# Seventy-three stores of a fused attention and feed-forward kernel, issued by GpSimd instead of SyncE

## The chip, the core and the metric

The kernel runs on one core of one Trainium2 chip. Time is device time in microseconds (us) of one execution; lower is better. Three runs before the change gave 1566.15, 1566.42 and 1566.45 us. All tensors are f32.

A core has five engines that the text calls by short names: PE (TensorE, matrix products), DVE (VectorE), ACT (ScalarE), POOL (GpSimd) and SP (SyncE, which here only starts transfers). Each engine takes its own instructions strictly in order, and waits on semaphores where it needs another engine's work. Transfers between SBUF and DRAM are run by 16 DMA engines; an engine's queue only starts them.

## The reference, cut to what matters

For x of shape (8, 512, 512), eight batches of 512 tokens by 512 features:

```python
xn = layernorm(x)
# attention: q, k, v = xn @ W.T + b; phi = elu + 1 on q and k
kv = cumsum(phi_k * v, axis=tokens)
s  = (phi_q * kv) * 32**-0.5 @ Wo.T + bo
# feed-forward: 512 -> 2048 -> 512 with Walsh-Hadamard transforms
h  = fwht(xn * SU_ug) / 64
h  = silu(h @ Wgate.T * scale_gate) * (h @ Wup.T * scale_up)
f  = fwht(h * SU_dp) / 64 @ Wdown.T * scale
out = x + s * silu(f)
```

The transforms are folded into the weights once, on the chip: a Hadamard transform of the input is the same as one of the weight matrix.

## The kernel before

The eight batches are worked on in four **pairs**. Every matrix product is done by a Strassen-Winograd scheme: seven products of half-size blocks in place of eight, at the price of additions on the blocks. Weights, activations and results therefore exist in seven **factors**, called P1 to P7; P1, P2, P7 and P4 come from the four quarters themselves and P5, P6, P3 and P7 are made by four additions or subtractions ("encoding").

**The first pair** is special: it uses the raw weights, folds and encodes them as it goes, and stores the made factors into DRAM. The other three pairs only load those factors. So nearly all the stores of weights happen in the first quarter of the run. In it:

- `first_w` (q, k, v and o weights): raw blocks are loaded by SP (`raw_w` L350, `rows_w` L367), encoded on POOL (L305 to L308), and `keep_w` (L317 to L321) stores them: 8 stores of 896 KB, 128 pieces of 7168 bytes each.
- `folded_w` (gate and up weights, each in 8 blocks `f`): raw load (L350), butterflies on DVE (L930 to L933), the Hadamard product on PE (L939), scaling on ACT (L945), encoding on DVE (L305 to L308).
- `inner_w` (L394 to L416) encodes a pair of folded blocks a second time. It stores three given factors at once (P1, P2, P4) and then makes P5, P6, P3 and P7 on DVE (L408), each stored when made. Each of these stores is 448 KB in 896 pieces of 512 bytes. P7 is written into the same third of the tile as P5 (`t[:, 0]`), so DVE's P7 has to wait until P5's store has landed. There are seven stores for each of gate and up in each of the four units `u`: 56 in all.
- `down`'s weights: `load_down` (L961), butterflies on DVE (L969, L974), Hadamard products on PE (L988), scaling on ACT (L994), and a store of the folded block into `wd_f` (L997): 4 stores of 1 MB in 512-byte pieces. `first_half_down` loads half of it back (L1008), makes the factors on DVE (L93) and stores them (L1018): 1 store of 3.5 MB. `down_w` does the other half block by block: loads (L367), factors on DVE (L93, L333), store (L388): 4 stores of 896 KB.

These 73 stores are the ones the change touches.

**Order.** A framework gives each engine its list of instructions, in the order of an estimated schedule with priorities, and inserts the semaphores. The kernel steers it: `at(place, fn)` sets a step that many PE groups ahead, `later` and `pace` hang small DVE steps behind given DVE instructions, and `background` lowers the priority of what can wait. All transfers but one are started by SP (the exception loads `cols` from ACT's queue). SP takes them in order, so a store that waits for its data holds all loads behind it. POOL starts no transfer: it does elementwise work, in the first pair the encoding of q, k, v and o weights, `v*k` (L716), the encoding of the attention result `co` and of the hidden units `ho` (L297 to L300, L793, L795).

Of the kernel before, what the change touches and what calls it, by code (L numbers as in the profile page):

```python
# [21 lines left out]
def kernel(  # L22
# [27 lines left out]
    nc = tc.nc  # L50
    P = 128
# [34 lines left out]
    def later(us, fn, *args, soon=False):  # L86
        (urgent if soon else idle).append((us, fn, args))
# [228 lines left out]

    def keep_w(name, w):  # L317
        d = dram.tile([P, 2 * 7 * P], F32, tag=f"d_{name}", name=f"d_{name}")
        nc.sync.dma_start(d, w.rearrange("p j s e -> p (j s e)"))
        kept[name] = d  # L320
        return w  # L321

# [33 lines left out]
    def by_factor(w, n=1):  # L356

        w = flat(w) if len(w.shape) == 4 else w
        w = w[:, : 7 * n * 2 * P] if n == 1 else w[:, : n * 2 * P]
        return w.rearrange("p (s e) -> p s e", e=2 * P)  # L360

    def rows_w(w, src, n0, dn):

        for a in range(2):
            for b in range(2):
                n = n0 + b * dn
                nc.sync.dma_start(  # L367
                    w[:, (P1, P2, P7, P4)[2 * a + b]], src[n * P : (n + 1) * P, a * 2 * P : (a + 1) * 2 * P]
                )

    wd_made = [0, 0]
    wd = [dram.tile([P, 7, 4, 2 * P], F32, tag=f"d_down_{h}", name=f"d_down_{h}") for h in range(2)]

    def down_w(u, j):

        t = t8.tile([P, 2, 7, P], F32, tag="t", name=f"wd_{u}_{j}")
        w = by_factor(t)
        rows_w(w, wd_f, u + NU * j, NG)

        def encode():  # L380
            for o, a, b, op in (
                (P5, P7, P4, ALU.add), (P6, P5, P1, ALU.subtract), (P3, P2, P6, ALU.subtract), (P7, P1, P7, ALU.subtract)
            ):
                later(0.5, nc.vector.tensor_tensor, w[:, o], w[:, a], w[:, b], op)
            later(0.0, store)

        def store():
            nc.sync.dma_start(wd[u // 2][:, :, 2 * (u % 2) + j], w)  # L388
            wd_made[u // 2] += 1

        at(8, encode)

    def inner_w(m, u, w0, w1):

        if u not in inner:
            inner[u] = dram.tile([P, 7, 2, 7, P], F32, tag=f"d_gu_{u}", name=f"d_gu_{u}")
        d = inner[u][:, :, ("gate", "up").index(m)]

        def store(c, t):
            nc.sync.dma_start(d[:, :, c, :], t)  # L400

        store(P1, w0[:, 0])
        store(P2, w0[:, 1])
        store(P4, w1[:, 1])
        t = xin.tile([P, 3, 7, P], F32, tag="x", name=f"s_{m}_{u}")

        def made(c, i, a, b, op):
            nc.vector.tensor_tensor(t[:, i], a, b, op)  # L408
            store(c, t[:, i])

        later(1.0, made, P5, 0, w1[:, 0], w1[:, 1], ALU.add, soon=True)
        later(1.0, made, P6, 1, t[:, 0], w0[:, 0], ALU.subtract, soon=True)
        later(1.0, made, P3, 2, w0[:, 1], t[:, 1], ALU.subtract, soon=True)
        later(1.0, made, P7, 0, w0[:, 0], w1[:, 0], ALU.subtract, soon=True)
# [7 lines left out]
    def at(place, fn):  # L422
        agenda.append((now[0] + place, now[1], fn))
        now[1] += 1
# [533 lines left out]
    wd_f = dram.tile([FF, D], F32, tag="wd_f", name="wd_f")  # L958
# [24 lines left out]
    def fold_down(o):  # L983
        r = rs[:, o % 2]
        for a in range(NF // 4):
            p = ps.tile([P, 4, P], F32, tag="t", name=f"pwd_{o}_{a}")
            tc.keep_in_program_order(
                nc.tensor.matmul(  # L988
                    p.rearrange("p c e -> p (c e)"), had,
                    r[:, 4 * a : 4 * a + 4].rearrange("p c e -> p (c e)"), start=True, stop=True,  # L990
                )
            )
            for c in range(4):
                nc.scalar.activation(  # L994
                    r[:, 4 * a + c], p[:, c], AF.Copy, scale=su_dp[:, 4 * a + c : 4 * a + c + 1]
                )
        nc.sync.dma_start(wd_f[:, o * P : (o + 1) * P].rearrange("(c p) e -> p c e", p=P), r)  # L997

    def first_half_down():

        n = 4 * 2 * P
        w = [rd[:, i * n : (i + 1) * n] for i in range(7)]
        for a in range(2):
            for b in range(2):
                t = w[(P1, P2, P7, P4)[2 * a + b]].rearrange("p (u j e) -> u p j e", u=2, j=2)
                d = wd_f[:, a * 2 * P : (a + 1) * 2 * P].rearrange("(b j u p) e -> b u p j e", b=2, j=2, p=P)
                for u in range(2):
                    nc.sync.dma_start(t[u], d[b, u])  # L1008

        def factors():  # L1010
            for i, x, y, op in (
                (P5, P7, P4, ALU.add), (P6, P5, P1, ALU.subtract), (P3, P2, P6, ALU.subtract), (P7, P1, P7, ALU.subtract)
            ):
                later(1.2, nc.vector.tensor_tensor, w[i], w[x], w[y], op, soon=True)
            later(0.0, at, 4, store, soon=True)

        def store():
            nc.sync.dma_start(wd[0].rearrange("p i k e -> p (i k e)"), rd)  # L1018
            wd_made[0] = 4

        at(8, factors)
# [4 lines left out]
    def first_w(m, g):  # L1026


        if m == "gate":
            return folded_w(m, wgate_t, g)  # L1030
        if m == "up":
            return folded_w(m, wup_t, g)
        name, eng = f"{m}_{g}", nc.gpsimd
        if m == "o":
            t = new_w(name)
            w = by_factor(t)
            rows_w(w, wo_t, g, 2)
        else:
            t = w = raw_w(name, sources[m], 0, 2, 1, g * P, 2 * P)

        def encode():
            encode_weights(eng, w)
            keep_w(name, t)

        return w, [(5, encode)]
# [73 lines left out]
    for i in range(7):  # L1119
        dst = had if i % 2 == 0 else had2  # L1120
        s = src.rearrange("p (a t h) -> p a t h", t=2, h=1 << i)
        d = dst.rearrange("p (a t h) -> p a t h", t=2, h=1 << i)
# [16 lines left out]
    rd = hop.tile([P, 2, 7, L], F32, tag="h", name="rd").rearrange("p m s t -> p (m s t)")  # L1139
# [9 lines left out]
    def chain_down(o):  # L1149
        def folded_block():  # L1150
            fold_down(o)
            if o + 2 < KD:
                at(8, lambda: load_down(o + 2))
            if o + 1 == KD:
                at(8, first_half_down)

        def then():
            at(10, folded_block)
            if o + 1 < KD:
                at(4, lambda: chain_down(o + 1))  # L1160

        butterflies_down(o, then)
# [116 lines left out]
```

## Time and profile before

| what | value |
|---|---|
| median of the three runs | 1566.42 us |
| the profiled execution's own time | 1564.62 us |
| span of its instructions | 1562.8 us |
| PE busy | 1529.4 us (98%) |
| DVE busy | 985.1 us (63%) |
| POOL busy | 497.5 us (32%) |
| ACT busy | 418.8 us (27%) |
| PE idle in 0 to 400 us / from 400 us on | 27.7 us / 5.9 us |
| POOL busy in 0 to 400 us | 130.2 us |
| bytes moved | 273.31 MB, mean 175 GB/s |

The page gives each engine's busy time and its share of the span, then 40 equal slices of the span with a digit for the busy tenths. "Waits" list who waited for whom: total us, number of times, longest. A window row gives the busy time of each engine in a stretch, the clock that the throttle granted to TensorE, the share in which the DMA engines were busy, and the GB/s. "To landing" is from a transfer's issue to its last byte's signal. SP's instructions are queue entries and not counted as busy.

### The profile page before, as it was taken

To read this page: it belongs to the slowest core of one execution; us is meant where nothing else is said; L and a number is where in the kernel's file an instruction comes from. 1 tells how busy PE (TensorE), PEld (TensorE's weight loads), DVE (VectorE), ACT (ScalarE), POOL (GpSimd) and SP (SyncE) were. 2 spreads that over 40 slices of the span, in tenths; PEclk is the share of its full clock that TensorE was granted. 3 is DMA by queue.
4 is the path that set the end of the run, shared out by engine and by line. 5 is a ranking of instruction groups with operands and counts; after the bars stand their busy time and mean duration, and the time that the engine had idled before them with its cause. 6 is when DMAs were issued, how large, how long until landed. Compare 5 with 4: busy or idle time off the path is not lost.

```text
span 1562.8 us, 15732 instructions
## 1 busy us (share of the span) xinstructions
PE 1529.4 (98%) x5924; PEld 1127.0 (72%) x5924; DVE 985.1 (63%) x1379; ACT 418.8 (27%) x664; POOL 497.5 (32%) x280
## 2 busy tenths in 40 slices
PE   7999999998999999999999999999999999999998
PEld 3335545845884588888885488888886468888887
DVE  5897785677866674716676574725675476543673
ACT  4443341142114521112215431111212431111211
POOL 4633144004321262304612235301622236110731
PEclk9999999999999999999999999999999999999999
DMA  8244867797785344344575434336474233535462
GB/s 280 78 153 152 268 218 225 232 275 270 200 304 196 91 158 155 108 152 165 157 286 213 102 137 148 135 102 195 153 249 171 85 106 117 185 99 177 155 260 85
DMA packets 197693, 273.31 MB, mean 175 GB/s; under 512 B 56817, under 2 KB 155121, under 8 KB 193393
## 3 DMA queue, kind: packets, MB, share of 16 engines
q1 hardware_dynamic: 197472, 272.27, 53.3%
q8 instruction: 47, 0.77, 0.2%
q14 instruction: 30, 0.24, 0.0%
q10 hardware_dynamic: 144, 0.03, 0.0%
HBM read 196.25 MB, written 76.02 MB: 174 GB/s over the span
## 4 chain that ended last, share of the span: by engine, by line
PE 88%; DVE 4%; DMA 3%; issue 2%; POOL 1%; ACT 1%; SPq 1%; POOLq 0%; DVEq 0%; ACTq 0%
PE px_gu L630 20%; PE px_dn L528 13%; PE pz_gu L630 10%; PE pz_dn L528 6%; PE py_gu L630 5%; PE py_dn L528 4%; PE px_k L452 3%; PE px_v L452 3%; PE px_o L528 3%; PE px_q L452 3%; PE pz_o L528 2%; PE pz_k L452 2%; PE px_gate L452 2%; PE pz_q L452 2%; PE pz_v L452 1%
## 5 line engine op out<-in xcount | busy, mean ns | idle before, releaser
L630 PE MATMUL px_gu<-xo,w_gu 128*128 128x256 f32 x1456 | 348.9, 381 | 0.0
L630 PEld LDWEIGHTS px_gu<-xo,w_gu 128*128 128x128 f32 x1456 | 277.5, 191 | 44.2 <-issue 5.0
L528 PE MATMUL px_dn<-w_down,ho 128*128 128x256 f32 x1024 | 228.9, 379 | 0.0
L528 PEld LDWEIGHTS px_dn<-w_down,ho 128*128 128x128 f32 x1024 | 194.9, 190 | 28.7 <-issue 2.9
L630 PE MATMUL pz_gu<-xo,w_gu 128*128 128x256 f32 x728 | 188.6, 382 | 5.4 <-DVE a L661 5.2
L831 POOL TENSOR_TENSOR u<-u,v 128x1024 f32<-128x1024 f32 x26 | 60.8, 2363 | 371.2 <-DVE u L668 347.5
L630 PEld LDWEIGHTS pz_gu<-xo,w_gu 128*128 128x128 f32 x728 | 138.3, 191 | 26.2 <-DVE a L661 6.1
L528 PE MATMUL pz_dn<-w_down,ho 128*128 128x256 f32 x496 | 112.4, 380 | 3.2 <-DVE u L468 3.2
L528 PEld LDWEIGHTS pz_dn<-w_down,ho 128*128 128x128 f32 x496 | 93.9, 190 | 17.0 <-DVE u L468 3.6
L630 PE MATMUL py_gu<-xo,w_gu 128*128 128x256 f32 x364 | 93.5, 379 | 0.0
L876 POOL TENSOR_TENSOR s<-s,d 128x512 f32<-128x512 f32 x30 | 40.0, 1333 | 165.5 <-ACT d L875 126.4
L716 POOL TENSOR_TENSOR v<-v,k 128x1024 f32<-128x1024 f32 x16 | 43.0, 2685 | 138.9 <-ACT v L691 111.2
L630 PEld LDWEIGHTS py_gu<-xo,w_gu 128*128 128x128 f32 x364 | 69.3, 190 | 9.3
L835 POOL TENSOR_TENSOR v<-v,r 128x1024 f32<-128x1024 f32 x26 | 60.9, 2362 | 27.7 <-DVE r L668 27.7
L793 POOL TENSOR_TENSOR ho<-g,u 128x512 f32<-128x512 f32 x6 | 10.9, 1812 | 161.0 <-DVE u L468 151.1
L452 PE MATMUL px_k<-xo,w_k 128*128 128x512 f32 x128 | 61.6, 603 | 0.0
L452 PE MATMUL px_v<-xo,w_v 128*128 128x512 f32 x128 | 60.8, 595 | 0.0
L821 ACT ACTIVATE a<-a,cols_sb 128x512 f32<-128x512 f32 x26 | 18.8, 722 | 155.2 <-DVE a L668 153.4
L452 PE MATMUL px_q<-xo,w_q 128*128 128x512 f32 x128 | 60.2, 593 | 0.0
L722 DVE TENSOR_TENSOR_SCAN k<-ones,v 128x512 f32<-128x512 f32 x32 | 40.9, 1317 | 28.6 <-POOL v L716 28.6
L528 PE MATMUL px_o<-w_o,co 128*128 128x256 f32 x256 | 58.4, 380 | 0.0
L875 ACT ACTIVATE d<-d 128x512 f32<-128x512 f32 x31 | 19.5, 630 | 144.5 <-DVE d L543 102.4
(264 smaller groups left out, 2476.5 us busy)
## 6 DMA issues: line engine op xcount, KB each, us to landing
w_gu<-d_gu SPq DMA_DIRECT2D x91, 896.0 KB, 4.4
w_down<-d_down SPq DMA_DIRECT2D x56, 512.0 KB, 3.6
d_s<-o SPq DMA_DIRECT2D x8, 1024.0 KB, 4.3
d_d<-dn SPq DMA_DIRECT2D x8, 1024.0 KB, 7.7
d<-d_d SPq DMA_DIRECT2D x8, 1024.0 KB, 6.2
s<-d_s SPq DMA_DIRECT2D x8, 1024.0 KB, 8.1
y<-in_x_dram SPq DMA_DIRECT2D x8, 1024.0 KB, 7.3
out_dram<-y SPq DMA_DIRECT2D x15, 512.0 KB, 3.3
```

What stands on the lines that cost most here:

```text
L452: nc.tensor.matmul(p.rearrange("p a t -> p (a t)") if len(r.shape) == 2 else p, ws[k][:, i, :], r, start=(first and k == 0), stop=(k == n ...
L528: nc.tensor.matmul(p[:, c], t[:, (2 * g + c) * P : (2 * g + c + 1) * P], ws[i](k), start=(first and k == 0 and c == cs[0]), stop=(k == n - ...
L630: nc.tensor.matmul(p[:, lane], w[:, lane, i, :], x[:, i, :], start=(first and lane == 0), stop=True, skip_group_check=True,)
L716: nc.gpsimd.tensor_tensor(v[:, h], v[:, h], k[:, h], ALU.mult)
L722: nc.vector.tensor_tensor_scan(k[:, h, s], ones.to_broadcast([P, L]), v[:, h, s], 0.0, ALU.mult, ALU.add)
L793: nc.gpsimd.tensor_tensor(ho[:, P1], g[:, 0, 0], r[:, 0, 0], ALU.mult)
L821: nc.scalar.activation(g[:, m], g[:, m], AF.Silu, scale=col("w_gate", u + m * NU + a * NG))
L831: nc.gpsimd.tensor_tensor(r[:, m], ru1[:, m], rv[:, m], ALU.add)
L835: nc.gpsimd.tensor_tensor(rv[:, m], rv[:, m], rr[:, m], ALU.add)
L875: nc.scalar.activation(d, d, AF.Silu)
L876: (nc.vector if final and (a, s) == (1, 0) else nc.gpsimd).tensor_tensor(r, r, d, ALU.mult)
```

## The change

Five `dma_start` calls are moved from SyncE's queue to GpSimd's. Nothing else is edited; the data, the sizes and the waits that each store needs are the same. The loads, the stores of normalized `x`, the parked results and the output stay on SyncE.

```diff
     def keep_w(name, w):
         d = dram.tile([P, 2 * 7 * P], F32, tag=f"d_{name}", name=f"d_{name}")
-        nc.sync.dma_start(d, w.rearrange("p j s e -> p (j s e)"))
+        nc.gpsimd.dma_start(d, w.rearrange("p j s e -> p (j s e)"))
...
         def store():                                   # down_w
-            nc.sync.dma_start(wd[u // 2][:, :, 2 * (u % 2) + j], w)
+            nc.gpsimd.dma_start(wd[u // 2][:, :, 2 * (u % 2) + j], w)
...
         def store(c, t):                               # inner_w
-            nc.sync.dma_start(d[:, :, c, :], t)
+            nc.gpsimd.dma_start(d[:, :, c, :], t)
...
-        nc.sync.dma_start(wd_f[:, o * P : (o + 1) * P].rearrange("(c p) e -> p c e", p=P), r)
+        nc.gpsimd.dma_start(wd_f[:, o * P : (o + 1) * P].rearrange("(c p) e -> p c e", p=P), r)
...
         def store():                                   # first_half_down
-            nc.sync.dma_start(wd[0].rearrange("p i k e -> p (i k e)"), rd)
+            nc.gpsimd.dma_start(wd[0].rearrange("p i k e -> p (i k e)"), rd)
```

## The prediction

> **What bounds the kernel now.** I read the page's busy line and slices first, then PE's waits, then the windows around each of them.
>
> ```profile
> PE 1529.4 (98%) x5924; PEld 1127.0 (72%) x5924; DVE 985.1 (63%) x1379; ACT 418.8 (27%) x664; POOL 497.5 (32%) x280
> ...
> PE   7999999998999999999999999999999999999998
> ```
>
> PE is busy for 98% of the span; all that an edit of queues can win is PE's idle time and what the throttle takes after it. The change acts on the first pair only, so the next view is the windows before and after 400 us:
>
> ```profile
> 0.00:400.00 400.00, 372.32 (x1076) 207.01 (x1077) 303.25 (x431) 139.82 (x269) 130.24 (x101) 0.97 0.68 213
> 400.00:1563.00 1163.00, 1157.07 (x4850) 920.01 (x4848) 681.87 (x949) 278.93 (x395) 367.29 (x180) 1.00 0.49 162
> 195.00:275.00 80.00, 76.79 (x211) 39.74 (x210) 57.67 (x81) 24.47 (x44) 36.11 (x21) 1.00 0.71 222
> 380.00:386.80 6.80, 3.72 (x9) 3.00 (x10) 6.52 (x12) 0.00 (x0) 1.82 (x2) 0.58 0.75 294
> ```
>
> The columns are the stretch, its length, busy us of PE, PEld, DVE, ACT and POOL, the granted clock, DMA share and GB/s. PE is idle for 27.7 us of the first 400 (8.3 of them before 40 us, while the first data arrive), and 5.9 us later. The last row shows a second price: after a stall of PE the clock was granted at 0.58 for some microseconds. Who ended PE's waits between 20 and 400 us:
>
> ```profile
> PE pz_gu L630 <- DVE a L661: 5.2, 1, 5.2
> PE pz_q L452 <- DVE q L468: 3.4, 1, 3.4
> PE pz_dn L528 <- DVE u L468: 3.2, 1, 3.2
> PE pwd L988 <- ACT w_gate L945: 3.2, 1, 3.2
> PE pz_o L528 <- DVE g L468: 2.9, 1, 2.9
> ```
>
> Five stalls carry 17.9 us: S1 at 55.9 us (pz_q), S2 at 105.9 (pwd), S3 at 142.9 (pz_o), S4 at 263.2 (pz_dn), S5 at 377.9 (pz_gu). Each time a PSUM bank is not yet read, because DVE or ACT is late. No stall names a transfer, so I ask next what made DVE late (DVE's waits, 0 to 400 us):
>
> ```profile
> DVE s_gate L408 <- DMA d_gu<-s_gate: 7.3, 2, 7.2
> DVE r_gate L930 <- DMA w_gate<-in_wgate_t_dram: 6.5, 2, 5.3
> ...
> DVE r_up L930 <- POOL ho L299: 6.1, 1, 6.1
> ...
> DVE wd L333 <- DMA wd<-wd_f: 4.6, 1, 4.6
> ```
>
> The first is 10 us ahead of S3, the second right ahead of S4, the fourth inside S5. In S5 SP's timeline shows the cause: a store (L388) held the queue until its data were made at 370.1 us, and the loads that DVE needs stood behind it and a second store.
>
> ```profile
> 361.73 0.61 SPq L327 DMA_DIRECT2D w_gu<-d_gu  x1
> 370.18 0.51 SPq L388 DMA_DIRECT2D d_down<-wd  x1
> 370.81 1.72 SPq L367 DMA_DIRECT2D wd<-wd_f  x2
> 372.63 0.52 SPq L388 DMA_DIRECT2D d_down<-wd  x1
> 373.50 1.77 SPq L367 DMA_DIRECT2D wd<-wd_f  x2
> ```
>
> S4 is alike: a store of s_up at 253.7 us waited for DVE, and seven raw loads of w_gate came after it at 255.0.
>
> **What is removed from SP.** 73 issues: 56 of L400 at a median of 0.52 us, 4 of L388 at 0.52, 4 of L997 at 0.37, 9 of L319 and L1018 at 0.34, together 36 us. SP is on no path by these; what counts is the waiting ahead of them.
> - S5: with the two L388 stores gone from the queue the four loads can start after 361.7 us, 9 us sooner, and DVE's wait of 4.6 goes. PE's 5.2 us of idle go, and the clock: PE ran from 383.1 to 386.8 at half speed, 3.7 us for 1.85 us of work. **-7.1.** Late next is DVE itself, which works through the xo and wd subtractions at 362 to 374 us without a wait.
> - S4: the load comes 4.7 us sooner, but P7 of s_up comes later (below). **-2.5.**
> - S3: DVE made P5 of s_gate at 122.1 us and stood at P7 until 132.3, because its store was issued at 125.1, behind two that waited (d_o for POOL, wd_f for ACT), and took 7.2 to land. On POOL it stands behind the last encoding of w_o (ends at 124.2): 124.2 + 2.4 + 3.0 = 129.6, 2.7 us sooner. **-2.7** of S3's 2.9.
> - S1 and S2 hang on v L716, the scans and DVE's order, and on no store.
>
> **What is added to POOL.** The trace of before has no transfer issued by POOL, so its time for one store is the unknown that decides. Below: SP's 0.52 for the same store. Above: 4.4, the median from issue to landing of the d_gu stores, if POOL were held as long as the whole transfer. Between them lies what POOL takes to pass over a tile of about this size, 2.36 (L835, 128x1024; the stored tile is 128x896). I take 2.4 for stores in 512- or 1024-byte pieces, the row nearest in size, and 1.3 (the usual row of 128x512) for the nine in whole rows: 64 x 2.36 + 9 x 1.27 = 162 us on top of the 130 that POOL works in 400 us. Laid out in the order in which data were ready in this trace, with POOL's own instructions at their times:
> - S1: d_v is ready at 45.7, as v L716 wants to start: +1.3 us on the chain v, scan, q to PE. **+1.3** (0.3 to 2.4).
> - Unit 1 (195 to 275 us) issues 14 stores of d_gu and the store of rd: 36.1 + 14 x 2.36 + 1.3 = 70 of 80 us. It fits; the limit is (80 - 36.1 - 1.3) / 14 = 3.0 us a store. From 237 us to L795 at 266.5, eight stores and 11 us of POOL's own work share 29.5 us: no delay up to 2.3 us a store. L795 and its followers L298 to L299 feed down's P2 and later products; PE takes P2 at 275.2 against 269.1 ready, which covers 6 us more.
> - P7 waits for P5's store: 3.0 us from issue to landing at best, plus POOL's time and queue. For s_up of unit 1: ready 247.4, POOL free at 249.9, landed at 255.3, against P7's start at 250.5 before. That is in S4's sum. In the other units DVE waits 0 to 2.5 us more, and waits of that size (3.3 at 219, 3.6 in the scans) preceded no idle of PE.
> - co (L298 to L300) is pushed back by up to 11 us at 126 to 130; PE takes its P6 some 20 us later. ho of unit 2 by 5 us at 362 to 382; POOL then idles for 17 us. Loads of made factors come 30 us or more after their stores (w_gu of unit 3 at 335.6 for use at 364), or in the second pair.
> - Waiting stores now hold POOL's work behind them, as they held SP's. That work (ho, co, v) mostly waits for the same late DVE, so I put it at nothing; where it does not, the price is a late ho, the first rival.
>
> Against the change speaks the Trainium skill, "DMA: Bandwidth & Descriptors", section "Issuing engines are not separate DMA queues": starting transfers from several engines saves only the sequencer's issue time, usually small. By that the gain would be nothing, since SP's 36 us are on no path; S5's row shows a queue that was held by a wait, which the sentence does not count. The same page, section "Latency and other measured facts", gives about 1 us to the first byte for a transfer from GpSimd and 0.6 from SyncE: 0.4 us more on each P7 wait if it holds, and no run here shows it yet.
>
> **The sum.** -7.1 - 2.5 - 2.7 + 1.3 = -11.0 us at 2.36 us a store. The framework will write another order for all engines, since its estimate of two queues changes; the first pair now has five stalls of 3.6 us on average plus some 1.4 of slow clock, and I allow one new one: +5. That gives -6 on the profiled execution's 1564.6, so 1558.6; the median of the three runs lies 1.8 above that execution: **1560.4**, about 1560.
>
> **Rivals.**
> 1. *POOL becomes the late engine* (slower). From 3.0 us a store on, unit 1 does not fit. At 2.8 my layout has L795 6 us late and P7 of s_up 9 us late; S4 stays and grows by 2, w_up's load (held until L795, which ended SP's longest load wait there) and so DVE at r_up by 6 to 10, of which the trace's pattern (6.1 us of such a wait cost nothing) leaves about 8 to PE, plus 3 of clock: with S5 gone about +6, and 1574. At 4.4 the first pair asks 304 + 130 = 434 us of POOL in 385: at least 50 longer, less S5, +40 or more, 1606. For it: 896 pieces a store, and POOL in program order. Against: POOL is idle from 273 to 343 us. Chance 0.32.
> 2. *The landing, not the issue*: stores and loads on two queues share the 16 DMA engines, 0.91 to 0.94 busy at 160 to 200 and 320 to 360 us; P5's stores take 7 us where they took 3 to 4, and DVE stands at P7 in all eight places. At 4 us each, with half of them reaching PE, +16, less 10: +6, 1572. Chance 0.12.
> 3. *Nothing to win*: most of the relief falls into 275 to 335 us, where PE is busy 60 of 60 us, and S4 and S5 come back in a new order. Within 3.1 us of 1566.4. Chance 0.12.
> 4. The forecast: faster, 1550 to 1563. Chance 0.44.
>
> **Range and chances.** A difference under 0.2% (3.1 us) can't be told from none. Faster 0.44; same 0.12; slower 0.32 + 0.12 = 0.44. The low end takes the lower bound of POOL's time (0.52 a store: -15 before the new stall): 1550. The high end takes in rival 1 up to about 4.4 us a store: 1605. The likeliest case alone spans 1550 to 1563.
>
> **What would show it.** In the new trace: POOL's mean for a d_gu store (below 2.5 right, above 3 wrong); the loads of wd at about 362 us and no wait of DVE at L333; no PE idle near 378; DVE's wait at P7 per unit (below 4 right); POOL's ho and co later by less than 10 us. A POOL that never idles in 195 to 275 us would be rival 1; short POOL times with landings of 7 us, rival 2. My sum is wrong at its root if POOL is held by each store's landing, or if the new order moves DVE's steps so that five other stalls appear.

## The result and the profile after

The changed kernel took 1573.57 us (median of 4 runs, 1572.81 to 1576.65) against 1566.43 for the kernel before in the same comparison: the ratio is 1.0044, with an interval of 1.0031 to 1.0057. It is 7.1 us slower where I had forecast 6 us faster. Its profiled execution took 1573.88 us, with a span of 1572.1; that of before took 1564.62.

The busy line of the page, and the stretch of unit 1 with the same columns as before:

```profile
PE 1533.1 (98%) x5924; PEld 1126.3 (72%) x5924; DVE 994.8 (63%) x1379; ACT 418.5 (27%) x664; POOL 562.0 (36%) x353
```

```profile
195.00:275.00 80.00, 72.91 (x180) 34.62 (x179) 62.77 (x79) 20.81 (x35) 41.63 (x33) 0.95 0.59 212
```

GpSimd worked 64.5 us more in all (562.0 against 497.5), and in the stretch from 195 to 275 us it is busy for 41.6 of 80 us: it is not the engine that became the bound. TensorE lost its time there: it was idle for 7.1 us in place of 3.2, and the granted clock fell from 1.00 to 0.95. Who ended PE's waits (20 to 400 us):

```profile
PE pz_o L528 <- DVE g L468: 5.8, 1, 5.8
PE px_gate L452 <- ACT sb_gate L462: 3.4, 1, 3.4
PE pwd L988 <- ACT w_gate L945: 3.2, 1, 3.2
PE pz_gu L630 <- DVE u L468: 3.0, 1, 3.0
PE pz_up L452 <- DVE u L468: 2.8, 2, 1.6
PE pz_q L452 <- DVE q L468: 2.6, 1, 2.6
PE pz_dn L528 <- POOL ho L300: 2.5, 1, 2.5
PE pz_gate L452 <- DVE g L468: 1.6, 1, 1.6
```

Eight groups with 24.9 us stand where five with 17.9 stood. S3 (pz_o) doubled, a stall at 216 us (px_gate) is new, S4 (pz_dn) now names GpSimd, and S5 came back as two smaller ones (pz_up, pz_gu).

TensorE's instructions come in the same order in both kernels, so the two traces can be laid side by side, matmul by matmul. How far the changed kernel lies behind, in us, and what each place added (half clock included):

| place | predicted | in the trace | behind by then |
|---|---|---|---|
| S1 and up to 135 us | +1.3 | -2.3 | -2.3 |
| S3, 135 to 148 us | -2.7 | +4.6 | +2.3 |
| new stall at 216 us | +5 (allowance) | +5.4 | +7.7 |
| S4, 260 to 278 us | -2.5 | +3.5 | +11.2 |
| S5, 375 to 395 us | -7.1 | -2.1 | +9.1 |

After 400 us nothing more is added. The 9.1 is that of the two profiled executions, which lie 9.3 apart; the medians lie 7.1 apart.

VectorE's waits (0 to 400 us) say where it was held:

```profile
DVE s_gate L408 <- DMA d_gu<-s_gate: 8.2, 3, 7.2
DVE r_up L930 <- DMA w_up<-in_wup_t_dram: 7.2, 2, 6.7
...
DVE s_up L408 <- DMA d_gu<-s_gate: 5.1, 1, 5.1
...
DVE s_up L408 <- DMA d_gu<-s_up: 3.7, 2, 3.5
```

The 6.7 us at r_up (until 283.5 us) cost nothing: PE has no stall after it. L408 writes P7 over P5 in the tile of made factors, and the next tile takes the same slot, so VectorE stands until a store has landed. With a group of 1.8 us further down, it did so for 18.8 us; before, the three such groups had 10.4. S3 shows why. GpSimd's timeline first:

```profile
125.37 2.12 POOL L299 TENSOR_TENSOR co<-co 128x512 f32<-128x512 f32 x1
127.43 1.21 POOL L997 DMA_DIRECT2D wd_f<-rd  x1
128.64 2.90 POOL L400 DMA_DIRECT2D d_gu<-s_gate  x3
```

ScalarE had made the data of L997 by 119.5 us and VectorE had made P5 by 122.2, but both stores stand behind the encoding of co (119.1 to 127.4) in GpSimd's order. P5 went out at 128.6 (before: 125.1) and landed at 134.6, and VectorE went on there:

```profile
134.62 1.09 DVE L408 TENSOR_TENSOR s_gate<-w_gate,w_gate 128x896 f32<-128x896 f32 x1 [7.17 <-DMA d_gu<-s_gate]
```

SyncE's timeline shows a second wait beside it:

```profile
104.64 1.78 SPq L367 DMA_DIRECT2D w_o<-in_wo_t_dram  x4
133.24 0.38 SPq L961 DMA_DIRECT2D rd<-in_wdown_t_dram  x1
135.78 7.06 SPq L350 DMA_DIRECT2D w_up<-in_wup_t_dram  x8
```

The queue that was to be freed stands still for 26.7 us: the load of rd (L961) overwrites what L997 stores and waits until it has landed, and the eight loads of w_up stand behind it. They go out at 135.8 us; before it was 135.5.

The wait ahead of the new stall at 216 us is of the first kind. VectorE's timeline:

```profile
196.86 1.09 DVE L408 TENSOR_TENSOR s_up<-w_up,w_up 128x896 f32<-128x896 f32 x1 [3.54 <-DMA d_gu<-s_up]
```

The place S4 needs its clock read beside its stalls. The rows of 260 to 278 us, with the columns of before: the kernel before, the changed kernel, and e5 of the experiments below, in which only L388 was moved:

```profile
260.00:278.00 18.00, 14.79 (x57) 10.47 (x56) 11.80 (x22) 4.39 (x10) 8.04 (x5) 1.00 0.47 139
260.00:278.00 18.00, 14.31 (x45) 9.41 (x44) 15.89 (x15) 0.16 (x1) 10.92 (x10) 0.81 0.52 169
260.00:278.00 18.00, 13.87 (x42) 9.22 (x41) 10.72 (x18) 4.27 (x10) 8.01 (x5) 0.81 0.39 112
```

TensorE's idle time there hardly grew (3.2 us before, 3.7 after). What was added is clock: 0.81 in place of 1.00. The kernel before was spared the half clock at S4, and e5, with every d_gu store still on SyncE, was not.

### The profile page after: what moved, and what is told of

It is laid out like the page before. It is cut to its first block, busy times and chain, and to the rows that moved or that the text cites. A ratio compares the mean times of both kernels' runs of the same rounds, so it can differ in the third digit from the quotient of the medians.

```text
span 1572.1 us, 15823 instructions
## 1 busy us (share of the span) xinstructions
PE 1533.1 (98%) x5924; PEld 1126.3 (72%) x5924; DVE 994.8 (63%) x1379; ACT 418.5 (27%) x664; POOL 562.0 (36%) x353
## 3 DMA queue, kind: packets, MB, share of 16 engines
q1 hardware_dynamic: 133200, 227.70, 44.2%
q0 software_dynamic: 10512, 44.57, 7.4%
## 4 chain that ended last, share of the span: by engine, by line
PE 84%; DVE 7%; DMA 3%; issue 2%; POOL 2%; ACT 1%; SPq 0%; POOLq 0%; DVEq 0%; ACTq 0%
PE px_gu L630 20%; PE px_dn L528 13%; PE pz_gu L630 10%; PE pz_dn L528 6%; PE py_gu L630 5%; PE py_dn L528 4%; PE px_o L528 3%; PE px_k L452 3%; PE px_v L452 3%; PE px_q L452 3%; PE pz_o L528 2%; PE px_gate L452 2%; PE pz_k L452 2%; DVE rd L969 1%; PE pz_q L452 1%
## 5 line engine op out<-in xcount | busy, mean ns | idle before, releaser
L821 ACT ACTIVATE a<-a,cols_sb 128x512 f32<-128x512 f32 x26 | 18.8, 722 | 155.2 <-DVE a L668 153.4
L528 PE MATMUL py_dn<-w_down,ho 128*128 128x256 f32 x256 | 57.9, 379 | 0.0
```

The costliest lines, as they stand in the source:

```text
L528: nc.tensor.matmul(p[:, c], t[:, (2 * g + c) * P : (2 * g + c + 1) * P], ws[i](k), start=(first and k == 0 and c == cs[0]), stop=(k == n - ...
L821: nc.scalar.activation(g[:, m], g[:, m], AF.Silu, scale=col("w_gate", u + m * NU + a * NG))
```

## The experiments

Five theories, by the letters used in the expectations. **A**: VectorE is held by landings of stores of made factors, which GpSimd issues late or which land late. **B**: GpSimd's own encodings stand behind its stores. **C**: only the new written order costs time, whatever the queue. **D**: SyncE stands at a load that waits for a moved store (L961 for L997). **E**, for S5: VectorE has no room at 362 to 385 us, so the stall comes back in another place. In the diffs `sync` and `gpsimd` are the queues. Each kernel was timed beside the kernel before on the same chip, whose median lay between 1566.0 and 1567.4; the ratios are to that.

| run | us | ratio (interval) |
|---|---|---|
| the change | 1573.57 | 1.0044 (1.0031 to 1.0057) |
| e1, only L400 moved | 1572.59 | 1.0033 (1.0020 to 1.0045) |
| e2, all but L400 | 1564.64 | 0.9987 (0.9977 to 0.9997) |
| e3, P5, P6, P3, P7 back | 1565.24 | 0.9994 (0.9985 to 1.0004) |
| e4, fourth place for P7 | 1567.02 | 1.0007 (0.9996 to 1.0018) |
| e5, only L388 moved | 1563.49 | 0.9975 (0.9966 to 0.9985) |
| e6, only P5, P6, P3, P7 moved | 1570.32 | 1.0018 (1.0010 to 1.0027) |
| e7, L997 back | 1569.71 | 1.0008 (0.9998 to 1.0018) |
| e8, P5, P6, P3, P7 and L997 back | 1561.07 | 0.9958 (0.9946 to 0.9970) |
| e9, three stores back | 1567.39 | 1.0013 (1.0000 to 1.0026) |
| e10, only L319 and L388 moved | 1559.27 | 0.9958 (0.9943 to 0.9974) |

**e1 and e2: which part carries the loss.**

```
e1: L400         sync -> gpsimd, the other four lines on sync
e2: L319, L388, L997, L1018  sync -> gpsimd, L400 on sync
```

> Only L400 (the factors of gate and up, 56 stores) goes from SyncE to GpSimd; L319, L388, L997 and L1018 stay on SyncE. Theory A (landings: VectorE is held at P7 and at the next tile by the landing of a GpSimd store of a made factor, in three places): the whole loss comes with L400. VectorE's waits at L408 for d_gu landings stay near the 17 us of the changed kernel (before: about 7 at s_gate), the stalls at 148, 216 and 270 us stay, and the stall at 378 us of the kernel before stays too, because L388 is still ahead of the loads of wd: 1574 to 1580 us. Theory B (GpSimd's own encodings stand behind its stores): also about 1574, but with a stall of PE that names GpSimd's ho or co and with short waits at L408. Theory C (only the new written order): anything, VectorE's order differs from before in 38 lines only, so the loss should be a third or less of 7 us: 1567 to 1569.

> L319, L388, L997 and L1018 (17 stores) go to GpSimd, L400 stays on SyncE. Theory A: the waits at L408 are as before (about 7 us at s_gate), the stall at 378 us is gone, none of the stalls at 148, 216 and 270 us grows: 1559 to 1563 us. Theory B: 17 stores take about 13 us of GpSimd, ho and co hardly move: 1559 to 1565. Theory C: VectorE's order differs from before in 77 lines, so a loss as in the changed kernel: 1570 to 1576.

The loss comes with L400 (e1, +0.33%); without it there is a small gain (e2, -0.13%). The order alone (C) is out as the main cause: e2 has twice e1's changed lines on VectorE and is not slower. The parts do not simply add up: +0.33% and -0.13% against +0.44% for the change. In e1 the stall S5 is there as before (5.2 us at pz_gu) and the waits at L408 for d_gu landings are 12.9 us (before 10.4, changed kernel 18.8; I had expected near 17). In e2 the gain of S5 is smaller than I expected; e5 takes that up. Against the expectation, e2 also has a stall of 2.4 us at px_gate near 213 us and one of 4.2 at pz_dn, though no store of L400 is on GpSimd in it.

**e3 and e6: the raw and the made factors.**

```
e3, from the changed kernel, in made():
-            store(c, t[:, i])
+            nc.sync.dma_start(d[:, :, c, :], t[:, i])
e6, from the kernel before:
+            nc.gpsimd.dma_start(d[:, :, c, :], t[:, i])
```

> As the changed kernel, but the stores of the made factors P5, P6, P3 and P7 go back to SyncE; the stores of P1, P2 and P4 and the other four kinds stay on GpSimd. Theory A: what VectorE waits for at L408 is back on SyncE's queue, so the waits at L408 fall from 17 to below 8 us and the stalls at 148 and 216 us go: 1560 to 1565 us. Theory B: GpSimd still issues 41 of the 73 stores and waits for VectorE in them, so half the loss stays: 1568 to 1572. Theory C: about as the changed kernel, 1570 to 1576.

> Only the stores of the made factors P5, P6, P3 and P7 (32 of the 56 of L400) go to GpSimd, all else stays on SyncE: the other half of the run that put these back. Theory A: the loss is here, 1570 to 1575, with waits at L408 of 15 us or more between 20 and 420 us. Theory B: 32 of 73 stores, less than half the loss: 1567 to 1569. Theory C: VectorE's order differs from before in 30 lines only: 1566 to 1568.

The 32 stores of made factors alone cost 0.18% (e6); with them back and the other 41 on GpSimd the loss is gone (e3). In e6 VectorE's waits at L408 are 17.0 us together, in e3 3.3. In e3 the wait at P7 in S3 is gone (P5 issued at 122.1, landed in 3.1 us), but VectorE then stood 2.2 us at L930 for the load of w_up, and 2.3 us of the stall at pz_o stayed, as did 1.8 us at px_gate near 210 us, against the expectation that both would go.

**e4: P7 in a place of its own.** It needs no landing any more; GpSimd's program stays.

```
-        t = xin.tile([P, 3, 7, P], ...)
+        t = xin.tile([P, 4, 7, P], ...)
-        later(1.0, made, P7, 0, w0[:, 0], w1[:, 0], ...)
+        later(1.0, made, P7, 3, w0[:, 0], w1[:, 0], ...)
-    snap = ctx.enter_context(tc.tile_pool(name="snap", bufs=6))
+    snap = ctx.enter_context(tc.tile_pool(name="snap", bufs=4))
```

> As the changed kernel, but the tile of made factors has a fourth place, so P7 doesn't overwrite P5 and needs no landing; the pool of snapshots is cut from 6 to 4 buffers to make the room. The next tile still reuses the one slot. Theory A: the waits at P7 (7.2 us before the stall at 148, 3.5 before the one at 216) go, the wait of s_up for the slot before 270 us stays; about 4 to 8 us are won on the changed kernel: 1565 to 1570 us. Theory B: GpSimd's program is nearly the same (18 lines), so is the time: 1572 to 1575. Theory C: the same as B.

It wins most of the loss back (1.0007), with GpSimd's program nearly the same, which speaks for A and against B. The new stall at 216 us is gone. S3 is not: it grew to 7.4 us. VectorE's timeline of e4 shows what was behind P7:

```profile
127.23 2.15 DVE L408 TENSOR_TENSOR s_gate<-w_gate,w_gate 128x896 f32<-128x896 f32 x1
...
145.60 0.69 DVE L930 TENSOR_TENSOR r_up<-w_up 128x512 f32<-128x512 f32 x1 [7.01 <-DMA w_up<-in_wup_t_dram]
```

P7 follows at once, and the same 7 us are lost 18 us later, at the load of w_up that SyncE issued at 134.8. For S3, A alone falls; that is where D came from.

**e7 and e8: the load behind the store.**

```
e7, from the changed kernel, L997:
-        nc.gpsimd.dma_start(wd_f[...], r)
+        nc.sync.dma_start(wd_f[...], r)
e8: e7 and e3 together
```

> As the changed kernel, with L997 (the stores of wd_f) alone back on SyncE. Theory D: at 104.6 us SyncE stands at the load of rd (L961), which overwrites what L997 stores, until that store has landed at 133.2, because L997 waits behind the encoding of co on GpSimd from 119.5, when its data are made, to 127.4; the eight loads of w_up behind it go out at 135.8 in the changed kernel. On SyncE the store goes out at about 119.6, the load of rd at about 126, the loads of w_up before 130; the P5 store of s_gate goes out on GpSimd at 127.4 in place of 128.6. The stall at 148 us shrinks from 5.8 to 2 to 4: 1569 to 1572 us. If A is the whole cause, only the 1.2 us of the P5 store are won: 1572 to 1573.

> As the run that put the made factors P5, P6, P3 and P7 back on SyncE, and L997 back there too; P1, P2, P4, L319, L388 and L1018 stay on GpSimd. Theories A and D together: no wait of VectorE at P7 and the loads of w_up before 130 us, so the stall at pz_o (2.3 us there) and the 3.4 us of half clock after it go: 1560 to 1563 us, below the kernel before. If D is wrong: 1565 as the run without L997.

With a ratio of 1.0008, returning the four stores of L997 alone takes back most of the loss, as e4 does in another way; the time lies in the expected range only because the kernel before took 1567.4 us beside it. In e7 the store goes out at 119.9, the load of rd at 125.0, the loads of w_up at 132.3 (I expected before 130). There is no wait at L930 any more, but P5 is still GpSimd's, VectorE stood 5.1 us at P7, and 2.9 us of the stall stayed. In e8 both are gone, and PE's waits there are:

```profile
PE pz_dn L528 <- DVE u L468: 4.1, 1, 4.1
...
PE pz_o L528 <- DVE g L468: 0.3, 1, 0.3
```

S3 is down to 0.3 us, and TensorE, 2.6 us ahead of the kernel before at the start of that stall, is 6.7 ahead behind it. The time is 0.42% below that kernel's. Two waits stood one behind the other; taking away either left the other.

**e9: three stores of 73.** The three on whose landing VectorE stood longest:

```
-            store(c, t[:, i])
+            (nc.sync if (m, u, c) in (("gate", 0, P5), ("up", 0, P5), ("gate", 1, P7))
+             else nc.gpsimd).dma_start(d[:, :, c, :], t[:, i])
```

> As the changed kernel, with three of its 73 moved stores back on SyncE: P5 of s_gate and of s_up in unit 0, and P7 of s_gate in unit 1, the three on whose landing VectorE stood for 7.2, 3.5 and 5.1 us. Theory A: the stall at 216 us and its half clock (5.4 us of the lag) go, s_up of unit 1 starts some 4 us sooner and the stall that names GpSimd's ho falls below 1.5 us; the stall at pz_o near 148 us stays at 2 to 7 us, because the loads of w_up still stand behind the load of rd (D): 1565 to 1568 us. Theory B: 70 of 73 stores are still GpSimd's, so little is won: 1571 to 1574.

The ratio falls from 1.0044 to 1.0013, some two thirds of the loss, with 70 of the moved stores still on GpSimd. PE's waits in e9:

```profile
PE pz_o L528 <- DVE g L468: 5.3, 1, 5.3
...
PE px_gate L452 <- ACT sb_gate L462: 2.0, 1, 2.0
...
PE pz_dn L528 <- DVE u L468: 1.6, 1, 1.6
```

S3 stays by D as expected, px_gate shrinks (2.0 is left, not nothing), and pz_dn no longer names GpSimd. That fits a late ho in S4 (B's share) that followed from VectorE's late s_up: the stores of s_up stood between ho's steps (L795, L298) on GpSimd because VectorE made their data late.

The place at 216 us depends on more than the queue of P5. Back on SyncE in e9, P5 of s_up (unit 0) still took 6.5 us to land, and 7.0 in e2. The twelve traces sort by L997 instead: 6.3 to 7.7 us where GpSimd issues it (the change, e2, e3, e4, e9), 4.7 to 5.8 in the seven where SyncE does. The loads of L1008 wait for L997's landing; the first of the four goes out 2.2 to 3.1 us ahead of P5's store in those five traces and 4.1 to 4.5 in the seven others. So D seems to have a part in this stall too, which goes with e7's gain. That the nearness of these loads makes the landing long was not tried by itself.

**e5: S5 by itself.**

```
-            nc.sync.dma_start(wd[u // 2][:, :, 2 * (u % 2) + j], w)
+            nc.gpsimd.dma_start(wd[u // 2][:, :, 2 * (u % 2) + j], w)
```

> Only L388 (the four stores of wd) goes from SyncE to GpSimd: the term S5 of the prediction by itself. As predicted: the loads of wd go out at about 362 us, PE's stall of 5.2 us at 378 and the half clock after it go: -7.1, 1559 us. Theory E (VectorE is full from 362 to 385 us; once the loads are early, its wd and layernorm steps are written ahead of the PSUM reads u L468 that PE waits for, so the stall comes back earlier and smaller): 2 to 3 us are won, a stall of 1 to 3 us at pz_up or pz_gu that names VectorE u L468: 1563 to 1564.5. Theory C (new order): VectorE's order differs in 67 lines, a loss: 1568 or more.

3.9 us were won (interval 2.4 to 5.3), not 7.1. VectorE's wait at L333 is gone, and PE waits like this near 378 us:

```profile
PE pz_gu L630 <- DVE u L468: 2.9, 1, 2.9
...
PE pz_up L452 <- DVE u L468: 0.7, 1, 0.7
```

VectorE's timeline of the kernel before has this:

```profile
374.33 0.68 DVE L468 TENSOR_TENSOR u<-sb_up,pz_up 128x512 f32<-128x512 f32 x1
379.58 2.85 DVE L333 TENSOR_TENSOR wd<-wd 128x256 f32<-128x256 f32 x3 [4.57 <-DMA wd<-wd_f]
```

The timeline of the changed kernel shows the same place, and what stands ahead of the read that pz_gu waits for:

```profile
386.12 0.76 DVE L333 TENSOR_TENSOR wd<-wd 128x256 f32<-128x256 f32 x2
386.80 0.68 DVE L794 TENSOR_TENSOR ho<-g,px_up 128x512 f32<-128x512 f32 x1
387.39 0.42 DVE L333 TENSOR_TENSOR wd<-wd 128x256 f32<-128x256 f32 x1
387.85 1.29 DVE L140 BATCH_NORM_STATS2 st<-x 128x6 f32<-128x512 f32 x2
...
389.53 0.65 DVE L468 TENSOR_TENSOR u<-sb_up,pz_up 128x512 f32<-128x512 f32 x1
```

In the kernel before, this read ran at 374.3, ahead of L333 and the layernorm steps, and those came after the wait. Now that the loads of wd are early (357.1 us in the changed kernel, with no wait at L333), the same work is written ahead of it. That it is the order, and not the amount, that brings the stall back was not tried by itself.

**e10: the small version.** Only the two kinds whose waiting held SyncE at S3 and S5.

```
L319, L388   sync -> gpsimd;  L400, L997, L1018 on sync
```

> Only L319 (8 stores of weight factors) and L388 (4 stores of wd) go to GpSimd; L400, L997 and L1018 stay on SyncE. With d_o gone from SyncE, which waited there for GpSimd until 124.2 us, L997 can go out at about 119.5 us and the P5 store of s_gate at 122, with P1, P2 and P4 still ahead of them on the queue. Theories A and D: the wait at P7 falls from 7.2 to below 3 us, the loads of w_up go out by 130 us, the stall at pz_o falls below 1 us and the lag from the stall at 378 us is as with L388 alone: 1560 to 1563 us, as the run with the made factors and L997 back. If the moved P1, P2 and P4 carried that gain: 1563 to 1564 as with L388 alone.

12 moved stores give 0.9958 (1559.27 us), the same as e8, and below both kernels. Its profiled execution took 1564.2 us, well above that median, so I read only its stalls: VectorE's wait at P7 is 1.9 us, no stall at pz_o is left, and S5 is as in e5. The loads of w_up went out at 134.5, not by 130 as I expected, and landed in time; of the two waits of S3 it is the one at P7 that fell here.

## Why the prediction was wrong

- **What bounds the kernel**: right. All that moved the time were PE's stalls in the first 400 us and the half clock after them, and each named VectorE or ScalarE as late, but for pz_dn in the change, e1, e4, e6 and e7, which names GpSimd's ho.
- **The sum**: -6 was forecast and +9.1 came in the trace. S3 missed by 7.3 us, S4 by 6.0 and S5 by 5.0; the stretch up to 135 us came out 3.6 better, and the allowance was used up (+5.4).
- **GpSimd's time for a store**: mis-sized, to my cost. I took 2.36 us; it measured 0.95 to 1.01 for L400 and L388, 1.19 for L997 and 0.57 to 0.66 for the whole rows. Summed over its groups that is 67.5 us, not 162. With that the first rival (GpSimd as the late engine) is out as the main cause. The kernel is slower all the same: the price of an issue does not decide here.
- **S3, -2.7**: the first step that failed. "On POOL it stands behind the last encoding of w_o" holds for when the data are ready, not for the order that was written: the store stood behind co's encoding and behind L997, went out at 128.6 in place of 124.2 and landed at 134.6, not 129.6. And I had named only the wait at P7; the load of w_up, which came at the same time as before, would have stopped VectorE a little later (e4). That a load on SyncE would stand until a moved store had landed (L961 for L997) is no term of the sum. Measured: +4.6.
- **S4, -2.5, and the P7 waits**: "3.0 us from issue to landing at best" was used as if it were usual. P7 of s_gate in unit 1 took 7.1 us in the changed kernel and 5.6 to 8.9 in the other four kernels that issue it from GpSimd (e1, e4, e6, e7), but 3.6 to 4.3 in the seven that issue it from SyncE. On SyncE the loads of w_down and w_gate stand behind the store; in the changed kernel they went out from 250.5 us on, beside a store issued at 250.7. The packet record of the changed kernel agrees: from 1.0 to 4.5 us after the issue no byte moves on GpSimd's queue, while SyncE's transfers keep the DMA engines busy (a share of 0.93 from 251.6 to 255.1 us); the store's 448 KB follow from 4.5 to 6.5 us. With SyncE's queue quiet a store's bytes move from 1.5 us after its issue and land in 3.3 us, also at 222.1 us, where GpSimd goes straight on to an encoding. That the shared DMA engines cause the difference stays argued from this; no run took those loads away. The next tile takes the slot, so s_up came late, and then ho, which PE's wait at pz_dn names. Of the loads of w_gate that were to go out sooner, four went out at 251.4 us and four only at 266.3. S4 became cheaper in none of the traces.
- **The clock at S4**: measured +3.5, but this is not shown to be the price of the late s_up. PE's idle time grew by 0.5 us, and the rest is 6.8 us of half clock from 270.9, which the kernel before was spared after a stall of 3.2 us. S4 adds 3.4 to 3.6 us in the same way in e2, e5, e8 and e10 (3.8 to 4.2 us at pz_dn behind VectorE, then 6.8 of half clock). Why the clock fell in one case and not in the other stays open.
- **S5, -7.1**: right mechanism, wrong size. The loads came early and the wait at L333 went; what I named as late next ("DVE itself") was put at nothing and cost some 3 us. The half clock behind S5 was also read short: it lasted to 387.8 us, not 386.8, 0.5 us more to win. Measured: -2.1 in the change's trace and -3.2 in e5's, whose median is 3.9 below the kernel before.
- **S1, +1.3**: measured -0.9 (the rest of the table's -2.3 lies before and behind it); the stall at pz_q is 2.6 us in place of 3.4, and no delay of v by the store of d_v reached PE.
- **The new stall, +5**: an allowance without a place; that its size came out (5.4, at px_gate) is luck: P5 of s_up in unit 0 took 7.7 us to land, before 4.7, and VectorE stood 3.5 us at P7.
- **The rivals**: the second is nearest: "short POOL times with landings of 7 us" is what the trace shows. I gave it 0.12 because I held the landings to be the same on either queue. It had all eight places; three carry some two thirds of the loss (e9). Part of S3 is neither rival: a store that stands behind GpSimd's own work, and a SyncE that stands at the load waiting for it.
- **The Trainium skill**: "DMA: Bandwidth & Descriptors", section "Issuing engines are not separate DMA queues", gives a saving of issue time alone. The change as a whole is no evidence against it: it saved nothing. e10's 6.7 us are not issue time: 12 issues of 0.34 to 0.52 us are 4.8 us together, on an engine off the path. They are waits taken from a queue.

## What to carry to other kernels

Before a store is moved to another queue, list who waits for its landing (the next write of its buffer, a load that refills it) and where it stands in the new engine's own order: a queue freed of waiting stores can stand just as long at the first load that depends on one. Move the stores whose data come late and whose landing nobody waits for soon; leave those on whose landing a buffer soon depends on the old queue, ahead of its loads (P7 of s_gate here: 3.6 to 4.3 us there, 5.6 to 8.9 on the other). And a stall that is removed is worth its length only after the late engine's other work at that place has been subtracted, and a comparison of two traces needs the granted clock at each place, since a stall of the same length had a half clock behind it in one and none in the other.

## What the runs showed of the hardware

The issue cost of a GpSimd store, one of GpSimd's groups in the changed kernel (columns: busy us, mean ns of one; then the idle time before them):

```profile
L400 POOL DMA_DIRECT2D d_gu<-s_up x16 | 15.3, 957 | 27.2 <-DVE s_up L408 25.0 <-DVE r_gate L931 1.6 <-issue 0.5
```

That is about twice SyncE's 0.52 us for L400; L997 with 1.19 us is three times SyncE's 0.37. Both are far from the 2.36 us that GpSimd takes to pass over such a tile. The DMA page has the 73 stores on a queue of their own:

```profile
q1 hardware_dynamic: 133200, 227.70, 44.2%
q0 software_dynamic: 10512, 44.57, 7.4%
```

10,512 packets are 144 a store; on SyncE's queue the same 44.57 MB made 64,272 (197,472 before, less 133,200). The larger packets did not land sooner: the shortest time from issue to landing was 3.3 us on GpSimd and 3.0 on SyncE. The 0.3 are near the difference of 0.4 that the Trainium skill gives in "DMA: Bandwidth & Descriptors", section "Latency and other measured facts" (about 1 us to the first byte against 0.6).

A VectorE instruction beside GpSimd's took a multiple of its time: L933 (0.69 us with GpSimd idle) took 4.65 at 267.0 us in the changed kernel, while GpSimd encoded ho (L298 to L299, 267.2 to 271.1), and 4.58 and 4.59 in e1 and e7, where the same steps met; in each of the three PE then stands 1.2 us at pz_up. In the other nine traces it took at most 1.75. It does not make up the loss as a whole: VectorE is busy for 306.3 us of the first 400 in the changed kernel, and for 311.4 in e8, one of the two fastest.
